# An earlier branch in a four-layer kernel's second layer, its planes' loads on three queues, and a gate product ahead of a reciprocal in the third

## The chip, the cores and the metric

The kernel runs on one core of one Trainium2 chip. Its engines are TensorE (PE, with its weight loads shown apart as PEld), VectorE (DVE), ScalarE (ACT), GpSimd (POOL) and SyncE (SP)[...]; SP, ACT and POOL also issue DMAs. The metric is the device time of one execution, in microseconds. Times come from three runs; the profile is of one further execution.

## What is computed

The input x is an image of 256 x 256 pixels with 128 channels, f32. Four layers are added to it one after the other, each on the group-normalised image:

```python
x = x + _L0_conv_ref(_gn(x), ...)   # triangle attention, 4 heads, gated
x = x + _L1_conv_ref(_gn(x), ...)   # triangle multiplication, 16 planes
x = x + _L2_conv_ref(_gn(x), ...)   # triangle multiplication, 128 planes
x = x + _L3_conv_ref(_gn(x), ...)   # shifts, taps and pixel-wise products
```

The change touches the second and the third of these (called layer 1 and layer 2 here, as in the code):

```python
def _L1_conv_ref(x, ...):
    a = jax.nn.sigmoid((x @ Wa1 + ba1) * (x @ Wa2 + ba2))
    b = jax.nn.sigmoid((x @ Wb1 + bb1) * (x @ Wb2 + bb2))
    g = jax.nn.sigmoid(x @ Wg + bg)
    z = jnp.einsum('bikc,bkjc->bijc', a, b)
    return g * (_ln(z, ln2_g, ln2_b) @ Wz + bz)

def _L2_conv_ref(z, ...):
    zn = _layernorm(z, ln_in_w, ln_in_b)
    a = jax.nn.sigmoid(zn @ Wga + bga) * (zn @ Wla + bla)
    b = jax.nn.sigmoid(zn @ Wgb + bgb) * (zn @ Wlb + blb)
    k = jnp.einsum('bimc,bmjc->bijc', a, b)
    return jax.nn.sigmoid(zn @ Wgo + bgo) * (_layernorm(k, ln_o_w, ln_o_b) @ Wlo + blo)
```

## The kernel before

Channels lie on the 128 partitions. The image is cut into 32 chunks (NSC) of 2048 pixels (SC), one f32 tile of 1 MB each; a chunk has four pieces of 512 pixels (CK). Between layers, x lies in DRAM (x1T after layer 0, x2T after layer 1, x3T after layer 2). Within the loops that matter here the order of instructions on each engine is the order in which the code issues them (`tc.manual_schedule()`).

Layer 1 has a first pass over all chunks (pool p3, line 944 on). `order1` (line 598) gives the order of the chunks. Every chunk has two sets of four matmuls of 128 x 32 by 512 (`piece_ab`, line 931, matmuls on line 937), an ACT addition (line 941), a DVE product (line 942), an ACT sigmoid (line 950), and one store of 256 KB into abD (line 951) that is issued one chunk later by POOL; the last chunk's is issued by SP. abD holds the 16 a planes and 16 b planes. The x tiles come from x1T on SP (`load1`, line 878, its DMA on line 881): eight chunks are there from layer 0, ten (NEAR) are loaded into left-hand slots before the pass, ten (FAR) into right-hand slots once the attention's memory is given up at the ninth chunk, and the last four reuse left-hand slots as soon as their chunks are done. So SP issues the load of the last chunk after the twelfth chunk's turn. Of the right-hand slots, seven (k from 3 to 9, `over_scope`) are given up at the end of the pass. Thirteen tiles (SLOTS, those of `order4[:SLOTS]`) stay in memory for layer 1's last pass (p4), which goes through the chunks in `order4`; that order is derived from `order1` by the list `after`.

After the pass comes a branch (lines 975 and 976): a flag, computed well before, says whether the statistics of layer 0 are usable. If they aren't, a general version of the attention is run, all chunks are done again, and the thirteen resident tiles are loaded anew; with these inputs this arm isn't taken. The branch is taken by all engines, each on its own.

Then the planes' products (pool z): for every pair of planes g, `load_z` reads A in four DMAs of 128 KB (line 1012) and B in two of 256 KB (line 1016) from abD. All are issued by SP, but for g = 0 ACT issues the two of B. PE transposes A's planes (line 2049) and multiplies (line 2060). The statistics over planes, layer 1's normalisation and the last pass follow.

Layer 2 computes its a and b planes into DRAM, and then the 128 products (p6): per plane, PE transposes and multiplies, ACT copies and squares, DVE adds to the sum k1 (line 1434), and POOL to the sum of squares k2 (line 1435). Its closing stage (p7, from line 1463) first makes the reciprocal standard deviation of k per pixel: k1 squared and scaled (line 1533, DVE), k2 + k1 (line 1534, DVE), max with 0 (line 1535, DVE), square root (line 1536, ACT), reciprocal (line 1537, DVE), a store of it to rkD and four loads of it as rows rk. Per chunk, a gate in two halves (`gate7`): two matmuls of 128 x 128 by 512 into a PSUM tile `p7_pm` of two buffers (line 1490), DVE adds a column and multiplies with rs2's row broadcast over partitions (line 1500), ACT takes the sigmoid. The broadcast (`spread_z`, line 1481, POOL's partition_broadcast on line 1484) has two buffers. The gates of chunks 0 to 2 stand ahead of the loop; `spread_k(0)` and `normalise_k` scale the first chunk of k, and in the loop PE does the gate three chunks ahead and the product of this chunk's k.

Of the kernel before, what the change touches and what calls it, by code (L numbers as in the profile page):

```python
# [8 lines left out]
F32 = mybir.dt.float32  # L9
AF = mybir.ActivationFunctionType  # L10
# [21 lines left out]
def kernel(ctx: ExitStack, tc: tile.TileContext, a: dict, out: bass.AP):  # L32
# [562 lines left out]

    order1 = [14, 15, 0, 16, 1, 17, 30, 31] + [b + h * NSC // 2 for b in range(2, NSC // 2 - 2) for h in range(2)]
    xs = {}

    def fill1(s, x):
# [265 lines left out]

    NEAR, FAR, FIRST = 10, 10, 8  # L870
    SLOTS = 13
    x1_scope, far_scope = ExitStack(), ExitStack()
    near = [
# [51 lines left out]
    usum = const.tile([P, 2 * NSC], F32, name="usum")  # L925
    qsum = const.tile([P, NSC], F32, name="qsum")

    after = [16, 17, 14, 15, 22, 23, 28, 29, 30, 31, 12, 13, 24, 25, 2, 3, 4, 5, 8, 9, 10, 11, 0, 6, 1, 7, 18, 19, 20, 21, 26, 27]
    order4 = [order1[i] for i in after]

    with x1_scope, far_scope:
# [10 lines left out]
            nc.vector.scalar_tensor_tensor(s1, p2, vb2, s1, ALU.add, ALU.mult)  # L942
            return s1, sb.tile([P, CK], F32, name="p3_ab", bufs=5)

        with tc.tile_pool(name="p3", bufs=2, reuse_waits="tile") as sb, tc.tile_pool(name="p3ps", bufs=3, space=PSUM, reuse_waits="tile") as ps, tc.manual_schedule():
            open_ab = []

            def close3(queue):
                s, s1, ab = open_ab.pop(0)
                nc.scalar.activation(ab, s1, AF.Sigmoid)  # L950
                queue.dma_start(abD[:, s * CK : (s + 1) * CK], ab)

            for i, s in enumerate(order1):
                if i == FIRST:
                    att_scope.close()
                    far = [
                        far_scope.enter_context(tc.tile_pool(name=f"x1_r{k}", bufs=1, side="right", reuse_waits="tile"))
                        for k in range(3)
                    ]
                    over_scope = ExitStack()  # L960
                    far += [
                        over_scope.enter_context(tc.tile_pool(name=f"x1_r{k}", bufs=1, side="right", reuse_waits="tile"))
                        for k in range(3, FAR)
                    ]
                    for m, k in enumerate((9, 4, 3, 8, 1, 0, 2, 7, 6, 5)):
                        load1(order1[FIRST + NEAR + m], far[k])
                open_ab.append((s, *piece_ab(s, sb, ps)))
                if i + NEAR + FAR < NSC and i >= FIRST:
                    load1(order1[i + NEAR + FAR], home[s])
                if i:  # L970
                    close3(nc.gpsimd)
            close3(nc.sync)
        over_scope.close()

        again = nc.values_load(flag[0:1, 0:1], min_val=0, max_val=1)
        with tc.If(again > 0):
            general_attention(
                tc, dict(xT=xT, rsD=rsD, mbD=mbD, triD=triD, x1T=x1T),
                dict(wf=wf, wo=wo, b_g=b_g, b_o=b_o, cqkg=cqkg, cv=cv, mneg=mneg, ident=ident),
                dram, stats1,  # L980
            )
            nc.vector.bn_aggr(mv1, stats1.rearrange("p n s -> p (n s)"))
            weights1("gn1g")
            with tc.tile_pool(name="g3", bufs=2, reuse_waits="tile") as sb, tc.tile_pool(name="g3ps", bufs=2, space=PSUM, reuse_waits="tile") as ps:
                held = dict(xs)
                for s in order1:
                    xs[s] = sb.tile([P, SC], F32, name="g3_x")
                    nc.sync.dma_start(xs[s], x1T[:, s * SC : (s + 1) * SC])
                    s1, ab = piece_ab(s, sb, ps)
                    nc.scalar.activation(ab, s1, AF.Sigmoid)  # L990
                    nc.sync.dma_start(abD[:, s * CK : (s + 1) * CK], ab)
                xs.update(held)
            for s in order4[:SLOTS]:
                nc.sync.dma_start(xs[s], x1T[:, s * SC : (s + 1) * SC])

# [3 lines left out]
        with tc.tile_pool(name="z", bufs=2, reuse_waits="tile") as sb, tc.tile_pool(name="zps", bufs=3, space=PSUM, reuse_waits="tile") as ps, tc.manual_schedule():  # L999
# [6 lines left out]
            def load_z(g):  # L1006
                if g < 8:
                    ab = gate_pool.tile([P, 4, 2 * N], F32, name="z_ab", tag="g")
                    AB[g] = A, B = ab[:, 0:2, :], ab[:, 2:4, :]
                    for q in range(4):  # L1010
                        r = slice(32 * q + 2 * g, 32 * q + 2 * g + 2)
                        nc.sync.dma_start(
                            A[32 * q : 32 * q + 32, :, :], abD[r, :].rearrange("c (s t) -> s c t", t=CK)
                        )
                    for c in range(2):
                        (nc.sync if g else nc.scalar).dma_start(
                            B[:, c, :], abD.rearrange("(q c) (s t) -> c s q t", q=4, t=CK)[16 + 2 * g + c]
                        )

# [372 lines left out]

    k1 = rk_pool.tile([P, 2 * N], F32, name="k1")
    k2 = rk_pool.tile([P, 2 * N], F32, name="k2")
    xs7 = {}

    def load7x(s):
        if s < NSC:
# [3 lines left out]
    with tc.tile_pool(name="p6", bufs=3, reuse_waits="tile") as sb, tc.tile_pool(name="p6ps", bufs=3, space=PSUM, reuse_waits="tile") as ps:  # L1402
        nc.vector.memset(k1, 0.0)
        nc.gpsimd.memset(k2, 0.0)  # L1404
        with tc.manual_schedule():
            quads = {}

            def load6(q):
                if q < D // 4:
                    A = sb.tile([P, 4, 2 * N], F32, name="p6_A")  # L1410
                    nc.sync.dma_start(A, aD[:, 4 * q : 4 * q + 4, :])
                    B = sb.tile([P, 4, 2 * N], F32, name="p6_B")
                    nc.sync.dma_start(B, bD[:, 4 * q : 4 * q + 4, :])
                    quads[q] = A, B

            def turn6(c):
                return tri_turn(nc, ps, sb, quads[c // 4][0], c % 4, ident, nc.vector.tensor_copy)

            for q in range(3):
                load6(q)  # L1420
            for s in range(4):
                load_row7(s)
            at = turn6(0)
            for c in range(D):
                q = c // 4
# [8 lines left out]
                nc.vector.tensor_tensor(k1, pz, k1, ALU.add)  # L1434
# [25 lines left out]
    g1 = const.tile([P, NSC + 1], F32, name="g1")  # L1460
    g2 = const.tile([P, NSC + 1], F32, name="g2")
    with tc.tile_pool(name="p7", bufs=2, reuse_waits="tile") as sb, tc.tile_pool(name="p7psX", bufs=2, space=PSUM, reuse_waits="tile") as psX, tc.tile_pool(name="p7psM", bufs=2, space=PSUM, reuse_waits="tile") as psM, tc.manual_schedule():
        ks, rks, rbs, gts = {}, {}, {}, dict(gates)
        junk = sb.tile([P, SC], F32, name="p7_junk", bufs=1)
        AHEAD = 3

# [14 lines left out]
        def spread_z(s):  # L1481
            if s < NSC and s not in gates:
                rbs[s] = sb.tile([P, SC], F32, name="p7_rb")
                nc.gpsimd.partition_broadcast(rbs[s], row7(s))

        def product7(src, w, h):
            pm = psM.tile([P, 2, CK], F32, name="p7_pm")
# [46 lines left out]
        nc.vector.tensor_tensor(k2, k2, k1, ALU.add)  # L1534
        nc.vector.tensor_scalar(k2, k2, 0.0, None, ALU.max)
        nc.scalar.activation(k2, k2, AF.Sqrt, bias=epst, scale=1.0 / D)
        nc.vector.reciprocal(k1, k2)
# [15 lines left out]
        for s in range(NSC):  # L1553
# [3 lines left out]
            for h in range(2):  # L1557
# [5 lines left out]
                )  # L1563
                if h == 0:
                    spread_k(s + 1)
                    spread_z(s + AHEAD + 1)
# [535 lines left out]
```

## The time and profile before

| what | us |
| --- | --- |
| median of three runs | 3238.36 |
| the runs | 3231.83, 3238.36, 3238.47 |
| the profiled execution | 3235.55 |
| its span, first to last instruction | 3233.8 |
| PE busy | 3052.5 (94%) |
| DVE busy | 2266.3 (70%) |
| ACT busy | 2035.2 (63%) |
| POOL busy | 1742.1 (54%) |

Layer 1's first pass begins at 1469.50 in the profile, its last store is issued at 1541.98, and the first planes' transposes begin at 1553.00. Layer 2's last plane product ends at 2596, and the closing stage's first matmul of the loop's steady work stands at 2620.33.

In the profile's lines, a time in front is the start in microseconds from the span's start, then the duration, the engine, the line of the code and the operation, what is written from what (output arrow input, with shapes), and how many instructions the line joins. A bracket gives the engine's idle time just ahead of it, and what ended that: the engine and instruction, or the DMA, that it waited for. An engine with a q (SPq) is its sequencer: DMA issues, branches and semaphore events, which don't count as busy. The mean granted TensorE clock over the span was 0.971 of full speed.

### The profile page before, as it was taken

Reading aid. Unit: us, or ns where it says so; the run is one execution under the profiler, and the core shown is the slowest. Engines: PE = TensorE matmul, PEld = TensorE weight load, DVE = VectorE, ACT = ScalarE, POOL = GpSimd, SP = SyncE. Lnnn points to the kernel's source line nnn. Section 1 sums busy time; section 2 is a strip of 40 time slices with the busy share of each in tenths; the row PEclk is TensorE's granted clock in tenths of the full one; section 3 lists DMA queues with packets and bytes.
Section 4 is the critical chain, followed back from the end, with each engine's and each line's share of the span. In section 5 each row is a group of like instructions: output and inputs, shape, how many; then the busy total and the mean of one; then the engine's idle time right before and its main releaser. Section 6 shows DMA issues by size and latency. Waiting matters only on the chain. (4 is left out here: it accounts for less than half of the span.)

```text
span 3233.8 us, 51742 instructions
## 1 busy us (share of the span) xinstructions
PE 3052.5 (94%) x19916; PEld 1629.4 (50%) x19916; DVE 2266.3 (70%) x2633; ACT 2035.2 (63%) x2275; POOL 1742.1 (54%) x951
## 2 busy tenths in 40 slices
PE   5699999999999999998798899999999989979998
PEld 4535555555555555552533344444699933324444
DVE  5657888888888888884456454455455578858887
ACT  3577777777777777764477544444344457757776
POOL 4006777777777777771277000000255568858887
PEclk8899999999999999999998899999999999989999
DMA  9973333333333333349589687676799989986885
GB/s 373 408 293 96 113 120 113 106 123 116 106 114 118 113 113 119 113 156 422 173 317 382 242 297 298 237 270 253 268 352 351 344 316 388 387 298 196 236 237 155
DMA packets 289526, 746.18 MB, mean 231 GB/s; under 512 B 68473, under 2 KB 139019, under 8 KB 240987
## 3 DMA queue, kind: packets, MB, share of 16 engines
q1 hardware_dynamic: 276881, 717.12, 62.1%
q0 software_dynamic: 8976, 23.49, 1.9%
q8 instruction: 159, 2.61, 0.3%
q10 hardware_dynamic: 3416, 2.19, 0.3%
q14 instruction: 94, 0.77, 0.1%
HBM read 455.26 MB, written 287.45 MB: 230 GB/s over the span
## 5 line engine op out<-in xcount | busy, mean ns | idle before, releaser
L679 POOL TENSOR_TENSOR p_es<-p_e 128x1024 f32<-128x1024 f32 x256 | 603.7, 2369 | 318.8 <-DMA p_x<-xT 195.7
L669 DVE TENSOR_TENSOR p_e<-p_S,tri_raw 128x1024 f32<-128x1024 f32 x512 | 609.4, 1212 | 143.4 <-PE p_S L659 142.0
L677 ACT ACTIVATE p_e<-p_e,mbT 128x1024 f32<-128x1024 f32 x512 | 552.1, 1138 | 62.1 <-DVE p_e L669 62.0
L1281 PE MATMUL p_pm<-p_zn,wf 128*128 128x512 f32 x1040 | 450.4, 595 | 1.9 <-ACT p_a L1342 1.9
L644 PE MATMUL p_mm<-p_xn,w 128*128 128x512 f32 x764 | 404.3, 612 | 0.1
L1281 PEld LDWEIGHTS p_pm<-p_zn,wf 128*128 128x128 f32 x1040 | 197.4, 190 | 255.0 <-issue 248.1
L659 PE MATMUL p_S<-p_qk 32*128 32x256 f32 x4096 | 295.4, 400 | 3.3 <-DVE p_e L669 3.3
L1404 POOL MEMSET k<- 128x512 f32 x1 | 0.5, 527 | 517.9 <-PE p_pm L1281 517.9
L659 PEld LDWEIGHTS p_S<-p_qk 32*128 32x128 f32 x4096 | 185.9, 184 | 159.2 <-PE p_mm L635 91.7
L2060 PE MATMUL tp_z<-p_B,tp_at 128*128 128x256 f32 x1024 | 250.6, 388 | 1.0 <-DVE tp_at L2051 1.0
L692 PE MATMUL p_o<-p_e,p_vg 128*32 128x256 f32 x4096 | 248.9, 384 | 0.0
L626 POOL TENSOR_TENSOR p_xn<-p_xn,p_rs 128x1024 f32<-128x1024 f32 x62 | 148.9, 2402 | 180.7 <-DMA p_rb<-rzD 119.6
L1435 POOL TENSOR_TENSOR k<-k,p_sq 128x512 f32<-128x512 f32 x128 | 163.2, 1275 | 136.4 <-ACT p_sq L1433 136.4
L2060 PEld LDWEIGHTS tp_z<-p_B,tp_at 128*128 128x128 f32 x1024 | 185.3, 191 | 23.7 <-DVE tp_at L2051 1.8
L1434 DVE TENSOR_TENSOR k<-tp_z,k 128x512 f32<-128x512 f32 x128 | 88.6, 692 | 127.5 <-ACT p_sq L1433 127.5
L644 PEld LDWEIGHTS p_mm<-p_xn,w 128*128 128x128 f32 x764 | 125.1, 190 | 103.6 <-issue 87.2
L692 PEld LDWEIGHTS p_o<-p_e,p_vg 128*32 128x32 f32 x4096 | 120.4, 110 | 110.4 <-ACT p_vg L650 41.5
L650 ACT ACTIVATE p_vg<-p_mm,bgh 128x512 f32<-128x512 f32 x128 | 88.0, 687 | 135.0 <-PE p_mm L644 135.0
L1431 ACT COPY p_K<-tp_z 128x512 f32<-128x512 f32 x128 | 75.0, 586 | 155.4 <-PE tp_z L2060 155.4
L1346 DVE SCALAR_TENSOR_TENSOR p_b<-p_pm,b2w,p_b 128x1024 f32<-128x1024 f32 x64 | 82.2, 1284 | 124.7 <-PE p_pm L1281 110.3
L635 PEld LDWEIGHTS p_mm<-w,p_xn 128*128 128x128 f32 x1016 | 133.9, 192 | 61.3 <-issue 60.6
L648 ACT ACTIVATE p_qk<-p_mm,cqkg 128x512 f32<-128x512 f32 x127 | 87.5, 689 | 122.5 <-PE p_mm L644 122.3
(417 smaller groups left out, 6094.0 us busy)
## 6 DMA issues: line engine op xcount, KB each, us to landing
p_x<-x2T SPq DMA_DIRECT2D x57, 1024.0 KB
x<-x1T SPq DMA_DIRECT2D x47, 1024.0 KB
p_x<-in_x_dram SPq DMA_DIRECT2D x32, 1024.0 KB
p_x<-xT SPq DMA_DIRECT2D x64, 512.0 KB
p_rs<-rsD SPq DMA_DIRECT2D x64, 512.0 KB
x2T<-x SPq DMA_DIRECT2D x32, 1024.0 KB
aD<-p_a SPq DMA_DIRECT2D x32, 1024.0 KB
bD<-p_b SPq DMA_DIRECT2D x32, 1024.0 KB
```

The source lines that it names most:

```text
L626: nc.gpsimd.tensor_tensor(xn, xn, groups[g]["rs"], ALU.mult)
L635: nc.tensor.matmul(pm[:, k * D : (k + 1) * D], lhsT=t["xn"][:, b * P : (b + 1) * P], rhs=wf[:, 2 * D : 3 * D], start=True, stop=True,)
L644: nc.tensor.matmul(pm, lhsT=w, rhs=t["xn"][:, cs_], start=True, stop=True)
L659: nc.tensor.matmul(Ss[h // 2][:, h % 2, u, :], lhsT=t["k"][hp, r * N + u * P : r * N + (u + 1) * P], rhs=t["q"][hp, r * N : (r + 1) * N], ...
L669: nc.vector.tensor_tensor(e[:, :, 2 * p : 2 * p + 2, :].rearrange("p u h n -> p h u n"), Ss[p], triT[:, 2 * p : 2 * p + 2, :, :], ALU.add,)
L677: nc.scalar.activation(e[:, u, :, :], e[:, u, :, :], AF.Exp, bias=mbT[:, u, i : i + 1])
L679: nc.gpsimd.tensor_tensor(es, e[:, 0, :, :], e[:, 1, :, :], ALU.add)
L692: nc.tensor.matmul(t["o"][hp, r % 2, :], lhsT=t["v"][:, r * 2 + u, hp], rhs=e[:, u, h, :], start=(u == 0), stop=(u == 1),)
L1281: nc.tensor.matmul(pm[:, c, :], lhsT=wf2[:, i, :], rhs=zns[s][:, k * CK : (k + 1) * CK], start=True, stop=True)
L1434: nc.vector.tensor_tensor(k1, pz, k1, ALU.add)
L1435: nc.gpsimd.tensor_tensor(k2, k2, sq, ALU.add)
L2060: nc.tensor.matmul(pz[:, t, :], lhsT=at[:, u, t * P : (t + 1) * P], rhs=Bc[:, u, :], start=(u == 0), stop=(u == 1))
```

## The change

- The order of chunks in layer 1's first pass: 30 and 31 change places with 1 and 17. The list `after` and the order in which the right-hand slots are filled are changed with it.
- The first pass becomes a function `pass_a(lo, hi, queue)`. It is called for the first 25 chunks (TAIL = NSC − 7), whose last store POOL issues; then the slots of `over_scope` are given up, the flag is read and the branch is taken; then it is called for the last seven chunks, whose last store SP issues. The arm that isn't taken repeats only the first 25 chunks, and loads the thirteen resident tiles anew as before.
- For g = 0 the planes' loads are spread: A's first two on SP, A's other two on ACT, B's two on POOL.
- Layer 2's closing stage: the first broadcast is made inside the plane loop, 16 planes before its end, in a buffer of its own, and the broadcasts then alternate between that buffer and one of the stage's. k2 + k1 goes from DVE to POOL, max with 0 from DVE to ACT as a Relu; the gate's first half for chunk 0 is put ahead of the reciprocal, its second half just behind it.

```diff
-    order1 = [14, 15, 0, 16, 1, 17, 30, 31] + [b + h * NSC // 2 for b in range(2, NSC // 2 - 2) for h in range(2)]
+    order1 = [14, 15, 0, 16, 30, 31, 1, 17] + [b + h * NSC // 2 for b in range(2, NSC // 2 - 2) for h in range(2)]
...
-    NEAR, FAR, FIRST = 10, 10, 8
+    NEAR, FAR, FIRST, TAIL = 10, 10, 8, NSC - 7
...
+        with tc.tile_pool(name="p3", bufs=2, reuse_waits="tile") as sb:
+            def pass_a(lo, hi, queue):
+                with tc.tile_pool(name=f"p3ps_{lo}", bufs=3, space=PSUM, reuse_waits="tile") as ps, tc.manual_schedule():
+                    open_ab = []
...
+                    for i in range(lo, hi):
+                        s = order1[i]
+                        if i == FIRST:
...
+                            for m, k in enumerate((9, 4, 3, 8, 7, 6, 5, 2, 1, 0)):
+                                load1(order1[FIRST + NEAR + m], far[k])
+                        open_ab.append((s, *piece_ab(s, sb, ps)))
+                        if i + NEAR + FAR < NSC and i >= FIRST:
+                            load1(order1[i + NEAR + FAR], home[s])
+                        if i > lo:
+                            close3(nc.gpsimd)
+                    close3(queue)
+
+            far, over_scope = [], ExitStack()
+            pass_a(0, TAIL, nc.gpsimd)
+            over_scope.close()
+            again = nc.values_load(flag[0:1, 0:1], min_val=0, max_val=1)
+            with tc.If(again > 0):
+                general_attention(
...
+                    for s in order1[:TAIL]:
...
+                for s in order4[:SLOTS]:
                     nc.sync.dma_start(xs[s], x1T[:, s * SC : (s + 1) * SC])
...
+            pass_a(TAIL, NSC, nc.sync)
...
-                        nc.sync.dma_start(
+                        (nc.sync if g or q < 2 else nc.scalar).dma_start(
                             A[32 * q : 32 * q + 32, :, :], abD[r, :].rearrange("c (s t) -> s c t", t=CK)
                         )
                     for c in range(2):
-                        (nc.sync if g else nc.scalar).dma_start(
+                        (nc.sync if g else nc.gpsimd).dma_start(
...
+    rb_pool = rs2_scope.enter_context(tc.tile_pool(name="rb7", bufs=1, side="right", reuse_waits="tile"))
...
+    def spread_z(s, pool):
+        if s < NSC and s not in gates:
+            rbs[s] = pool.tile([P, SC], F32, name="p7_rb", bufs=1)
+            nc.gpsimd.partition_broadcast(rbs[s], row7(s))
...
                 nc.gpsimd.tensor_tensor(k2, k2, sq, ALU.add)
+                if c == D - 16:
+                    spread_z(0, rb_pool)
...
-        spread_z(0)
-        spread_z(1)
-
         nc.vector.scalar_tensor_tensor(k1, k1, -1.0 / D, k1, ALU.mult, ALU.mult)
-        nc.vector.tensor_tensor(k2, k2, k1, ALU.add)
-        nc.vector.tensor_scalar(k2, k2, 0.0, None, ALU.max)
+        nc.gpsimd.tensor_tensor(k2, k2, k1, ALU.add)
+        nc.scalar.activation(k2, k2, AF.Relu)
         nc.scalar.activation(k2, k2, AF.Sqrt, bias=epst, scale=1.0 / D)
+        spread_z(1, sb)
+        gate7(0, 0)
         nc.vector.reciprocal(k1, k2)
+        gate7(0, 1)
...
         for s in range(3):
-            gate7(s, 0)
-            gate7(s, 1)
+            if s:
+                gate7(s, 0)
+                gate7(s, 1)
             if s < 2:
-                spread_z(s + 2)
+                spread_z(s + 2, (rb_pool, sb)[s % 2])
```

More of the change, by code (lines that the diff above doesn't have):

```diff
@@ L926 @@
     qsum = const.tile([P, NSC], F32, name="qsum")
-    after = [16, 17, 14, 15, 22, 23, 28, 29, 30, 31, 12, 13, 24, 25, 2, 3, 4, 5, 8, 9, 10, 11, 0, 6, 1, 7, 18, 19, 20, 21, 26, 27]
+    after = [16, 17, 14, 15, 26, 27, 28, 29, 30, 31, 12, 13, 25, 24, 2, 3, 6, 7, 8, 9, 10, 11, 0, 4, 1, 5, 18, 19, 20, 21, 22, 23]
     order4 = [order1[i] for i in after]
@@ L943, in piece_ab @@
             return s1, sb.tile([P, CK], F32, name="p3_ab", bufs=5)
[L945 to L987, printed above, removed]
-                    nc.sync.dma_start(xs[s], x1T[:, s * SC : (s + 1) * SC])
[L989 to L994, printed above, removed]
+        with tc.tile_pool(name="p3", bufs=2, reuse_waits="tile") as sb:
+            def pass_a(lo, hi, queue):
+                with tc.tile_pool(name=f"p3ps_{lo}", bufs=3, space=PSUM, reuse_waits="tile") as ps, tc.manual_schedule():
+                    open_ab = []
+                    def close3(queue):
+                        s, s1, ab = open_ab.pop(0)
+                        nc.scalar.activation(ab, s1, AF.Sigmoid)
+                        queue.dma_start(abD[:, s * CK : (s + 1) * CK], ab)
+                    for i in range(lo, hi):
+                        s = order1[i]
+                        if i == FIRST:
+                            att_scope.close()
+                            for k in range(FAR):
+                                scope = far_scope if k < 3 else over_scope
+                                far.append(scope.enter_context(
+                                    tc.tile_pool(name=f"x1_r{k}", bufs=1, side="right", reuse_waits="tile")
+                                ))
+                            for m, k in enumerate((9, 4, 3, 8, 7, 6, 5, 2, 1, 0)):
[12 more added lines that the diff above has]
+                general_attention(
+                    tc, dict(xT=xT, rsD=rsD, mbD=mbD, triD=triD, x1T=x1T),
+                    dict(wf=wf, wo=wo, b_g=b_g, b_o=b_o, cqkg=cqkg, cv=cv, mneg=mneg, ident=ident),
+                    dram, stats1,
+                )
+                nc.vector.bn_aggr(mv1, stats1.rearrange("p n s -> p (n s)"))
+                weights1("gn1g")
+                with tc.tile_pool(name="g3", bufs=2, reuse_waits="tile") as sb_g, tc.tile_pool(name="g3ps", bufs=2, space=PSUM, reuse_waits="tile") as ps:
+                    held = dict(xs)
+                    for s in order1[:TAIL]:
+                        xs[s] = sb_g.tile([P, SC], F32, name="g3_x")
+                        nc.sync.dma_start(xs[s], x1T[:, s * SC : (s + 1) * SC])
+                        s1, ab = piece_ab(s, sb, ps)
+                        nc.scalar.activation(ab, s1, AF.Sigmoid)
+                        nc.sync.dma_start(abD[:, s * CK : (s + 1) * CK], ab)
+                    xs.update(held)
+                for s in order4[:SLOTS]:
+                    nc.sync.dma_start(xs[s], x1T[:, s * SC : (s + 1) * SC])
+            pass_a(TAIL, NSC, nc.sync)
@@ L1394 @@
     k2 = rk_pool.tile([P, 2 * N], F32, name="k2")
-    xs7 = {}
+    xs7, rbs = {}, {}
+    def spread_z(s, pool):
+        if s < NSC and s not in gates:
+            rbs[s] = pool.tile([P, SC], F32, name="p7_rb", bufs=1)
+            nc.gpsimd.partition_broadcast(rbs[s], row7(s))
     def load7x(s):
@@ L1462 @@
     with tc.tile_pool(name="p7", bufs=2, reuse_waits="tile") as sb, tc.tile_pool(name="p7psX", bufs=2, space=PSUM, reuse_waits="tile") as psX, tc.tile_pool(name="p7psM", bufs=2, space=PSUM, reuse_waits="tile") as psM, tc.manual_schedule():
-        ks, rks, rbs, gts = {}, {}, {}, dict(gates)
+        ks, rks, gts = {}, {}, dict(gates)
         junk = sb.tile([P, SC], F32, name="p7_junk", bufs=1)
@@ L1479, in normalise_k @@
                 nc.vector.tensor_tensor(ks[s][:, hs], rks[s][h], ks[s][:, hs], ALU.mult)
[L1481 to L1484, printed above, removed]
         def product7(src, w, h):
@@ L1565 @@
                     spread_k(s + 1)
-                    spread_z(s + AHEAD + 1)
+                    spread_z(s + AHEAD + 1, (rb_pool, sb)[s % 2])
                 normalise_k(s + 1, h)
```

## The prediction

> **What bounds the kernel now.** I read the page first: PE is busy 94% of the 3233.8 us span, so a change in the order of work can only win where PE stands still. The table of windows then priced the two stages that the change touches, and the timelines of both showed which wait ends last. The table's columns are PE, PEld, DVE, ACT and POOL busy with their counts, then granted clock, DMA share and GB/s:
>
> ```profile
> 1469.50:1517.00 47.50, 46.91 (x400) 11.87 (x400) 16.73 (x24) 29.89 (x45) 11.41 (x21) 0.94 1.02 422
> 1517.00:1542.00 25.00, 13.47 (x112) 3.48 (x112) 7.43 (x10) 12.66 (x20) 5.43 (x11) 1.00 0.85 351
> 1542.00:1553.00 11.00, 0.00 (x1) 0.03 (x1) 0.48 (x1) 0.00 (x0) 0.00 (x0) 0.56 0.66 176
> 2597.90:2609.50 11.60, 3.75 (x9) 1.49 (x9) 10.64 (x7) 2.66 (x4) 5.97 (x3) 0.80 0.96 364
> 2620.30:2700.00 79.70, 79.70 (x240) 31.22 (x237) 71.16 (x60) 54.75 (x52) 61.76 (x19) 1.00 0.94 362
> ```
>
> Layer 1's first pass has its inputs early up to 1517. Its last seven chunks go at the pace of the loads (13.47 us of PE in 25), and then comes an 11 us hole. Layer 2's closing stage opens with PE at 3.75 of 11.60 us; after that PE is full. The end of layer 1's pass:
>
> ```profile
> 1535.32 1.92 PE L937 MATMUL p<-x,v 128*32 128x512 f32 x16 [1.63 <-DMA x<-x1T]
> ...
> 1538.51 1.92 PE L937 MATMUL p<-x,v 128*32 128x512 f32 x16 [1.27 <-DMA x<-x1T]
> ...
> 1541.33 0.63 ACT L950 ACTIVATE p_ab<-p_s 128x512 f32<-128x512 f32 x1 [0.43 <-DVE p_s L942]
> 1541.98 0.33 SPq L951 DMA_DIRECT2D abD<-p_ab  x1
> 1546.22 1.24 ACTq L1016 DMA_DIRECT2D z_ab<-abD  x2
> 1546.28 0.48 DVE L1026 MEMSET z_Z<- 128x512 f32 x1 [4.99 <-SPq L976]
> 1546.71 3.95 SPq L1012 DMA_DIRECT2D z_ab<-abD  x8
> ...
> 1553.00 1.95 PE L2049 MATMUL tp_a<-ident,z_ab 128*128 128x128 f32 x8 [12.57 <-DMA z_ab<-abD]
> ```
>
> Each chunk waits for its own load, the last computes at once, and then the branch and the planes' loads stand alone: 1541.96 to 1553.00 is 11.04 us. The view of the branch's line says what SP does in it:
>
> ```profile
> L976 SPq EVENT_SEMAPHORE  x8: 17/17/17, 1545.5 to 1546.1; - x8
> L976 PEldq COMPARE_BRANCH  x1: 3416/3416/3416, 1539.2 to 1539.2; - x1
> ...
> L976 SPq COMPARE_BRANCH  x1: 50/50/50, 1542.4 to 1542.4; - x1
> ```
>
> Eight semaphore events of SP follow its branch: one for each of its eight DMA counters. In the closing stage of layer 2:
>
> ```profile
> 2597.95 3.70 PE L1490 MATMUL p_pm<-p_x,wf 128*128 128x512 f32 x8 [1.90 <-DVE k L1434]
> 2598.56 5.30 POOL L1484 PARTITION_BROADCAST p_rb<-rs__18576  x2
> 2599.24 2.47 DVE L1534 TENSOR_TENSOR k<-k,k 128x512 f32<-128x512 f32 x1
> 2601.74 2.41 DVE L1535 TENSOR_SCALAR k<-k 128x512 f32<-128x512 f32 x1
> ...
> 2604.93 3.35 DVE L1537 RECIPROCAL k<-k 128x512 f32<-128x512 f32 x1 [0.79 <-ACT k L1536]
> 2608.20 2.38 DVE L1500 SCALAR_TENSOR_TENSOR p_g<-p_pm,gcol,p_rb 128x1024 f32<-128x1024 f32 x2
> ...
> 2609.45 9.88 PE L1490 MATMUL p_pm<-p_x,wf 128*128 128x512 f32 x16 [7.79 <-DVE p_g L1500]
> ```
>
> PE has two gate products and no free PSUM buffer; DVE gets to their release only behind the reciprocal, so PE idles 7.79 us.
>
> [...] chunks took 3.42 us each at the pass's start (1469.50 to 1475.2) and 1.72 when warm (two chunks, 1482.52 to 1485.95). [...] here eight issues took SP 3.95 us. [...]
>
> **Part 1, the branch seven chunks earlier.** Meant: branch and events hidden under the loads. But the program of the changed kernel, built and not run, has this in the arm not taken: SP waits for all DMAs that it has issued, on each of its eight counters, and only then adds what the other arm would have counted. Line 881 issues the last x load at 1510.3, before the branch, so the wait covers the last load. And PE's first matmul of chunk 25 waits for a counter's value *after* that addition, since the other arm loads the resident x tiles anew. So chunks 25 to 31 can't start with their own loads; all wait until the last has landed. Queued behind SP's wait: only the last ab store and the planes' loads, later anyway.
>
> - Last load: before, 1538.4 (PE starts at 1538.51). The stalled chunks put two or three ab stores of 256 KB fewer ahead of it; at 422 GB/s each is 0.62 us, 1.2 to 1.9 in all. I take 1536.9.
> - Burst of seven chunks: 7 × 1.72 = 12.0 us. PE has stood idle about 20 us and starts cold: 5.7 us at 3.42 a chunk do what 2.85 do warm, 2.85 more. ACT needs 0.69 + 0.63 = 1.32 a chunk, less than PE. PE ends at 1551.8, the last ab, 1.5 later as before, at about 1553.4 instead of 1541.96: **+11.4**. Bounds: +9 if the load comes earlier and PE warms sooner, +13 if the load is as late as before.
>
> **Part 2, planes on three queues, after the branch.** Of the 11.04 us, the branch goes (last store to first plane load was 4.24 us at ACT; a lone store lands 2.3 us after issue by its line's view, so about 2.0 of it is branch). Three issuers with two loads each instead of SP's first four in 2.0 us and more save 1.0 to 1.6. I take 11.04 − 3.5 = **7.5 us, −3.5**; bounds −2 and −4.5. Layer 1 nets +7.9.
>
> **Part 3, the closing stage.** The two broadcasts lay beneath DVE's 2.47 and 2.41; the same forms undisturbed took 0.69 (L1052) and 0.43 (L1054). One moves into the product loop: 2.3 to 2.65 us of POOL, whose slack is 2.27 − 1.27 = 1.0 an iteration with three buffers to lag in: nothing, +1 if not. Chain now: DVE's first product ends 2599.13; POOL's add 1.27 (L1435) in place of 2.47; ACT's Relu about 0.63 (128x512, L950) in place of 2.41; sqrt's table load 1.28, formerly hidden (it began at 2597.20), now lies behind Relu at worst; sqrt 0.72; reciprocal. It ends about 2606.6 instead of 2608.28. The first gate half goes on DVE at 2600.05, frees a PSUM buffer, and PE does the third half product early; the second goes at 2606.6 to 2607.85. PE restarts there, instead of at 2609.45, with three half products done instead of two (one cold: about 1.7). Together −3.3; PE is full afterwards (the row from 2620.30), so this reaches the end. Bounds −2 (Relu and tables slower, cold anyway) and −6.5 (clock stays warm). What is late next: the reciprocal's row through DRAM, store to use; it lands about 2612.5, before its use at some 2616.0, so nothing.
>
> The swap in order1, the derived orders and far slots exchange equal loads: nothing; the loads cover them (DMA share 1.02). If an order made one chunk of layer 1's closing stage late, up to +2.
>
> **Sum.** +11.4 − 3.5 − 3.3 = **+4.6 us**. On the profiled execution, 3235.55 us (span 3233.8 and 1.75 around it), that is 3240.2; the median of the runs is 3238.36, 2.81 above it, so 3243.0. The kernel's measurements can tell about 0.2% from no change, 6.5 us.
>
> **Rivals.**
> - *Slower: the second planes land late on POOL's queue.* In the DMA view POOL's 256 KB issues take 9.0 (ab stores) and 10.6 us (p_z) to land, ACT's z loads came within 6.9 of issue. Against it: those were taken on saturated queues, here DMA is nearly idle. It decides once a landing exceeds 6.9 us: 2 to 4.3 us more for the first product, +8.9 in all with the rest, 3247.3. Chance 0.27.
> - *The seven chunks do stream with their loads*, the wait of SP not holding PE. For it: before, each chunk waited for its own load alone. Against it: the counters' values in the built program. Then only −3.5 and −3.3: −6.8, 3231.6. Chance 0.10.
> - *The clock stays warm in the closing stage, or the burst starts sooner.* PE's longest idle there falls to about 4.65 us[...]. +1 to +2 net, about 3239.8. Chance 0.11.
>
> **How the numbers follow.** Forecast 0.52: 3243.0, by its bounds 3238 to 3247. Range: down to 3234, between the third and second rivals, up to 3250 for the first rival with late ends. Within 0.2% (3231.9 to 3244.8) I put 0.40 of the forecast's 0.52, 0.02 of the first rival, 0.05 of the second and 0.06 of the third: 0.53. Slower: 0.10 of the forecast and 0.25 of the first rival, 0.35. Faster: 0.02 of the forecast, half of the second rival, and 0.05 of the third, since the runs before themselves reach down to 3231.83: 0.12.
>
> **What would show it.** In the changed trace PE should stand idle from about 1516 to 1537 in the pass, then do seven chunks without a wait; if each of the last seven again names its x load, part 1 is wrong. From the last ab to the first plane product should be 7 to 8 us; over 9, with POOL's load as releaser, is the first rival. In the closing stage a gate half stands before the reciprocal and PE restarts 1.6 us earlier; if the first broadcast delays the product loop, or a table load stands twice, part 3 is smaller. Wrong altogether: a change in the stages outside these two of over 2 us.

## The result, and the profile after

| | before | changed |
| --- | --- | --- |
| median of 20 runs, us | 3235.55 | 3242.62 |
| lowest and highest, us | 3229.11, 3241.39 | 3233.97, 3246.82 |
| profiled execution, us (span) | 3235.55 (3233.8) | 3233.97 (3231.8) |

The ratio of changed to before is 1.0019, with a 95% interval from 1.0013 to 1.0026: 4.2 to 8.4 us slower. With twenty runs the kernel before has a median 2.81 us lower than with the three that were known at first. And the changed kernel's profile is of the quickest of its twenty executions. So the two spans must not be set against each other; stages are.

I take two distances inside each trace, since everything that the change touches lies in them: from the first pass's first matmul to the first planes' transposes, and from the start of the last matmul of layer 2's plane products to the first broadcast of rk's rows. Before, they are 83.5 and 23.6 us. In the changed kernel they are 91.1 and 20.2: **+7.6 and −3.4, +4.2 together**.

What PE waited for in the changed kernel between 1500 and 1560 us (engine, tile and line waited with, what ended it, us in all, times, longest):

```profile
PE p L937 <- SPq L977: 20.9, 1, 20.9
PE tp_a L2055 <- DMA z_ab<-abD: 8.0, 1, 8.0
```

In place of many short waits for x there is one of 20.9 us, and the profile names SP's branch as what ended it. The windows of the changed kernel, in the columns used before:

```profile
1465.80:1518.70 52.90, 46.82 (x400) 11.83 (x400) 18.88 (x26) 33.19 (x50) 12.52 (x24) 0.92 1.02 421
1518.70:1533.90 15.20, 0.03 (x4) 0.06 (x5) 0.00 (x0) 0.63 (x1) 1.06 (x2) 0.50 0.84 347
1533.90:1548.90 15.00, 14.98 (x112) 4.17 (x112) 4.51 (x6) 7.47 (x13) 2.71 (x5) 0.81 0.19 72
1548.90:1556.90 8.00, 0.00 (x0) 0.02 (x1) 1.24 (x2) 1.08 (x2) 1.64 (x3) 0.77 0.66 215
```

25 chunks (400 matmul records; the trace has two for each of a chunk's eight matmuls), then nothing on PE while the loads still run at 347 GB/s, then seven chunks in one go (112 records in 15.0 us) while the loads are over (72 GB/s). The 15.2 us of the second row are the part of PE's wait behind its own branch; the wait of 20.9 us begins at 1513.0. Loads and matmuls, which lay beside each other before, now stand one behind the other. The second row's granted clock is 0.50, and the burst's mean 0.81: 0.50 in its first 5.40 us (28 records) and 0.99 in the other 9.60 (88). Such a slow start is called cold below, also where an experiment's times alone show it. The branch's own line in the changed kernel:

```profile
L977 SPq EVENT_SEMAPHORE  x8: 17/17/17, 1516.8 to 1534.1; - x8
L977 SPq COMPARE_BRANCH  x1: 50/50/50, 1507.5 to 1507.5; - x1
L977 PEldq COMPARE_BRANCH  x1: 6272/6272/6272, 1512.5 to 1512.5; - x1
```

SP branches at 1507.5, but the last of its eight counters is settled at 1534.1, 26.6 us later. The first five events lie 3.5 to 3.7 us apart, the pace at which the loads let the chunks through before; the last three stand at 1533.6 to 1534.1, when the loads are over (16 and 33 GB/s in the two half microseconds from 1532.0, nothing from 1533.0 on). PE starts at 1533.87, behind the seventh. The closing stage in the changed kernel's timeline:

```profile
2596.07 1.20 DVE L1535 SCALAR_TENSOR_TENSOR k<-k 128x512 f32<-128x512 f32 x1
...
2597.41 1.26 POOL L1536 TENSOR_TENSOR k<-k,k 128x512 f32<-128x512 f32 x1 [0.69 <-DVE k L1535]
2598.16 1.28 DVE L1505 SCALAR_TENSOR_TENSOR p_g<-p_pm,gcol,p_rb 128x1024 f32<-128x1024 f32 x1 [0.90 <-PE p_pm L1495]
2598.70 0.63 ACT L1537 ACTIVATE k<-k 128x512 f32<-128x512 f32 x1 [3.40 <-POOL k L1536]
...
2599.35 1.28 ACT L1538 ACT_TABLE_LOAD   x1
...
2601.47 3.35 DVE L1541 RECIPROCAL k<-k 128x512 f32<-128x512 f32 x1 [2.02 <-ACT k L1538]
...
2605.98 8.05 PE L1495 MATMUL p_pm<-p_x,wf 128*128 128x512 f32 x12 [4.48 <-DVE p_g L1505]
```

The half gate stands ahead of the reciprocal. In place of DVE's steps of 2.47 and 2.41 us there are POOL's of 1.26 and ACT's Relu of 0.63, with no table load ahead of the Relu. PE pauses 4.48 us instead of 7.79, with 12 matmul records left to do behind the pause instead of 16.

### The profile page after: what moved, and what is told of

Read it like the earlier page. It is cut to its first block, busy times and chain, and to the rows that moved or that the text cites. A ratio compares the mean times of both kernels' runs of the same rounds, so it can differ in the third digit from the quotient of the medians.

```text
span 3231.8 us, 51747 instructions
## 1 busy us (share of the span) xinstructions
PE 3048.1 (94%) x19916; PEld 1627.6 (50%) x19916; DVE 2260.7 (70%) x2631; ACT 2037.6 (63%) x2276; POOL 1743.2 (54%) x954
## 3 DMA queue, kind: packets, MB, share of 16 engines
q10 hardware_dynamic: 3288, 1.93, 0.2%
## 5 line engine op out<-in xcount | busy, mean ns | idle before, releaser
L659 PE MATMUL p_S<-p_qk 32*128 32x256 f32 x4096 | 295.1, 400 | 3.3 <-DVE p_e L669 3.3
```

The costliest lines, as they stand in the source:

```text
L659: nc.tensor.matmul(Ss[h // 2][:, h % 2, u, :], lhsT=t["k"][hp, r * N + u * P : r * N + (u + 1) * P], rhs=t["q"][hp, r * N : (r + 1) * N], ...
```

## The experiments

The first two columns are the two distances in each kernel's trace, the third what they add up to against the kernel before (83.5 + 23.6); the last is the ratio of runs to those of the kernel before on the same chip. At some 3233 us, 0.001 is 3.2 us. Kernels without a ratio were run once, so that only their traces are read. e1 and e5 leave out reloads that the arm that isn't taken needs; they serve as experiments only.

| kernel | pass to planes | planes to rk | sum against before | ratio, 95% interval |
| --- | --- | --- | --- | --- |
| changed | 91.1 | 20.2 | +4.2 | 1.0019 (1.0013 to 1.0026) |
| e1_noreload | 83.6 | 19.2 | −4.3 | 0.9988 (0.9978 to 0.9997) |
| e2_arm_on_pool | 89.2 | 19.2 | +1.3 | 1.0013 (1.0004 to 1.0021) |
| e3_tail31 | 83.5 | 19.2 | −4.4 | 0.9988 (0.9982 to 0.9995) |
| e4_closing_stage_only | 83.5 | 19.2 | −4.4 | 0.9983 (0.9975 to 0.9990) |
| e5_noreload_own_ab | 81.5 | 19.2 | −6.4 | 0.9986 (0.9979 to 0.9993) |
| e6_layer1_only | 91.1 | 23.6 | +7.6 | 1.0032 (1.0022 to 1.0041) |
| e7_branch_behind_pass | 82.4 | 19.2 | −5.5 | 0.9988 (0.9979 to 0.9997) |
| e8_tail28 | 85.7 | 19.2 | −2.2 | |
| e9_order_only | 83.3 | 23.5 | −0.3 | 1.0001 (0.9993 to 1.0010) |
| e10_two_queues | 96.3 | 19.2 | +8.4 | 1.0041 (1.0027 to 1.0055) |
| e11_no_lead_gate | 83.3 | 21.1 | −2.7 | |
| e12_planes_as_before | 92.2 | 19.2 | +4.3 | |

**e1_noreload: what does PE wait for, the branch or a merged counter?**

```diff
-                for s in order4[:SLOTS]:
-                    nc.sync.dma_start(xs[s], x1T[:, s * SC : (s + 1) * SC])
             pass_a(TAIL, NSC, nc.sync)
```

> The changed kernel with the arm that is not taken left without its thirteen reloads of the resident x tiles (that arm alone would compute with old tiles). SP's wait on its eight counters in the branch stays. Theory (PE waits for counter values that only the branch's addition reaches, because the arm reloads tiles of the last seven chunks): each of the last seven chunks waits for its own load again; from the pass's first matmul to its last about 70 us as before, instead of 82.5; first planes' product about 79.5 us after the pass's start instead of 91.1 (83.5 before); against the kernel before -4 there and -3.4 in the closing stage, -7.4 us or 0.9977. Rival (the branch itself holds PE until SP is through it, whatever the arm contains): PE stands idle for 15 us before the seven chunks as in the changed kernel, ratio 1.0019.

83.6 us instead of the expected 79.5. The theory's direction holds, but of the 11.6 us that it set against the changed kernel 7.5 came, and the timeline says why:

```profile
1526.46 10.74 PE L937 MATMUL p<-x,v 128*32 128x512 f32 x80 [10.24 <-DVEq L977]
1537.72 0.63 ACT L952 ACTIVATE p_ab<-p_s 128x512 f32<-128x512 f32 x1 [5.72 <-SPq L977]
```

PE is no longer held by SP's branch: it starts the last chunks at 1526.46, once DVE is through its own branch, and does five of them (80 matmuls). But now ACT waits for SP's branch, before the first sigmoid of the last seven chunks. The arm that isn't taken takes its ab tiles from the pass's pool and stores them by SP; so the next user of such a tile waits for a counter value that only SP's branch brings. The merged wait sat in two places, and I had seen one.

**e5_noreload_own_ab: both taken away.**

```diff
-                        s1, ab = piece_ab(s, sb, ps)
+                        s1, ab = piece_ab(s, sb_g, ps)
```

(on top of e1's edit; the arm's pool `sb_g` was there already for its x tiles)

> The kernel of e1_noreload (the arm not taken does without its thirteen reloads), and that arm takes its ab tiles from a pool of its own, so that no store of that arm stands between ACT and the pass's ab tiles. Theory (every tile that the arm's DMAs touch too makes its next user wait for SP's whole branch): ACT no longer stops for about 6 us before the sigmoids of the last seven chunks; the pass streams; first planes' product 79 to 80 us after the pass's start (83.6 in e1, 91.1 in the changed kernel, 83.5 before); -4 there and -4.3 in the closing stage, about -8 us against the kernel before, 0.9975. Rival (ACT was held by the branch itself): as e1, 83.6 us and 0.9988.

```profile
1527.71 14.36 PE L937 MATMUL p<-x,v 128*32 128x512 f32 x112 [10.59 <-DVEq L977]
```

All seven chunks now go without a stop, and ACT's 5.72 us are gone: SP's branch holds nobody, though its last counter is settled only at 1538.2. That is 81.5 us, 9.6 less than the changed kernel, against 79 to 80 expected: PE still stands idle for 10.59 us; in that time PE's own branch takes 6.23 us and DVE's next event comes 5.6 us after its branch (last section). From the last ab store's issue (1543.63) to the planes' transposes (1552.19) are 8.6 us (7.8 in e1) where the changed kernel took 6.5; I didn't follow that up.

**e2_arm_on_pool: the same wait moved to another engine.**

```diff
-            nc.sync.dma_start(...)      # all DMAs of general_attention and of the arm's chunks and reloads
+            nc.gpsimd.dma_start(...)
```

> The changed kernel with all DMAs of the arm that is not taken issued by POOL instead of SP. Theory: SP has nothing to wait for in the branch, POOL waits for its own ab stores, the last of which lands about 9 us after its issue; PE gets chunk 25 about 4 us earlier than in the changed kernel and does a burst whose end is set by its own length: first planes' product about 87 us after the pass's start instead of 91.1, +0 to +1 us against the kernel before (1.000 to 1.0005). Rival (the branch itself holds PE until the last x load): no change from the changed kernel, 1.0019.

89.2 us where 87 was expected. SP has no waits in the branch any more; PE's idle time before the burst is 19.40 us, and POOL's ab stores are named as what ended it:

```profile
1533.03 14.21 PE L937 MATMUL p<-x,v 128*32 128x512 f32 x112 [19.40 <-DMA abD<-p_ab]
```

```profile
L977 POOLq EVENT_SEMAPHORE  x4: 17/43/43, 1522.4 to 1528.7; - x4
...
L977 POOLq INC_SWDGE_SEM  x1: 2131/2131/2131, 1530.8 to 1530.8; - x1
```

POOL issued its last store ahead of the branch at 1521.13, and the pass's ab stores by POOL take 9.0 us to land at the median and at most 9.9 in the changed kernel's trace, so by estimate it was there between 1530 and 1531. At 1530.8 POOL begins the 2.13 us of its INC_SWDGE_SEM, and PE starts 0.1 us after their end. So PE seems to have waited for POOL's branch as it waited for SP's before, and these 2.13 us, which the expectation had not counted, are the 2.2 that it missed. By the traces of the two kernels, the issuer of the DMAs of an arm that was not taken decided whose outstanding DMAs the following work waited for: SP's for 20.9 us, POOL's for 19.4.

**e3_tail31 and e8_tail28: how many chunks stand behind the branch.**

```diff
-    NEAR, FAR, FIRST, TAIL = 10, 10, 8, NSC - 7
+    NEAR, FAR, FIRST, TAIL = 10, 10, 8, NSC - 1
```

(NSC − 4 in e8_tail28)

> The changed kernel with one chunk behind the branch instead of seven. Theory: the chunks before the branch stream with their loads, the last one waits for the last load, which it needs anyway; nothing is left of the burst, PE's own branch of 3.4 us delays the last chunk by about 2; first planes' product about 80.5 us after the pass's start (91.1 in the changed kernel, 83.5 before); with the closing stage -6 us against the kernel before, 0.9981. Rival (the cost lies in the branch's place among the loads, not in the number of chunks behind it): still about 90 us, ratio 1.0015 to 1.002.

> The changed kernel with four chunks behind the branch instead of seven. Theory (burst behind the last load, cold at first): the four chunks start about 68.5 us after the pass's start and take about 9.7 instead of 15.0 us; first planes' product about 86 us after the pass's start. Rival (the wait doesn't depend on the number of chunks): 89 to 91 us.

Seven, four and one chunk behind the branch give 91.1, 85.7 and 83.5: the cost shrinks with what stands behind the branch. e8's distance came as expected (86), its course not quite. The first of its four chunks waits for DVE's branch alone and starts 64.1 us after the pass's start, cold (3.64 us, where a chunk ahead of the branch took 1.92); only the last three wait for SP's counters and go in one burst (70.5 us after the pass's start, 7.05 us long). e3 missed by 3 us (80.5 expected), because the branch comes back at the end:

```profile
1546.96 3.39 PE L937 MATMUL p<-x,v 128*32 128x512 f32 x16 [4.53 <-ACTq L977]
```

The last chunk waits 4.53 us for ACT's way through the branch, and runs cold (3.39 us, against 1.92 or 1.93 for the chunks ahead). The branch was not hidden; it moved ahead of one chunk. A chunk of e3 that stands ahead of the branch warns of the profile's label:

```profile
1530.02 1.93 PE L937 MATMUL p<-x,v 128*32 128x512 f32 x16 [1.46 <-SPq L977]
```

PE's own branch stands at 1541.5, and so this chunk can't wait for it; it waits for its load, whose landing lets SP's branch (events from 1526.5 to 1544.1) go on at the same time. So the label alone doesn't tell a wait for SP's branch from one for a load; e1 does.

**e4_closing_stage_only and e6_layer1_only: each half alone.**

e4 is the kernel before with the diff's second half, e6 the changed kernel with that half taken back:

```diff
+                if c == D - 16:
+                    spread_z(0, rb_pool)
...
-        nc.vector.tensor_tensor(k2, k2, k1, ALU.add)
-        nc.vector.tensor_scalar(k2, k2, 0.0, None, ALU.max)
+        nc.gpsimd.tensor_tensor(k2, k2, k1, ALU.add)
+        nc.scalar.activation(k2, k2, AF.Relu)
...
+        gate7(0, 0)
         nc.vector.reciprocal(k1, k2)
+        gate7(0, 1)
```

> The kernel before with the closing stage's part of the change alone. Theory: from the last plane product to the first broadcast of rk's rows 20.2 us instead of 23.6, and all of it reaches the end: -3.4 us, 0.9990. Rival (the gain is given back in the loop behind it, which PE or the loads of x bound): 0.9998 to 1.0002.

> The changed kernel with the closing stage of layer 2 as before. Theory: first planes' product 91.1 us after the pass's start instead of 83.5, +7.6 us against the kernel before, 1.0023. Rival (the medians of the changed kernel, +7.07, and of the closing stage alone, -5.5, differ by 12.6, so some 4 to 5 us more lie in other stages, from the new order of chunks): +11 to +12.6 us, 1.0034 to 1.0039, with a stage outside these two that is 4 us longer.

e4 gains 4.4 us in its stage, and 0.0017 (5.5 us) by the runs: the gain reaches the end. The stage is at 19.2 us in every other kernel with the whole of this closing stage; the changed kernel's own profile, at 20.2, is the exception (what PE does behind its pause took 8.05 us there and 7.11 in e4). e6 loses 7.6 us in its stage; 1.0032 is 10.3 us, with 7.1 to 13.3 in the interval, so its lower end holds the stage's loss and the rival's 11 to 12.6 is not excluded by the runs (e9 tests the rival's reason). The halves are opposite in sign, and the larger is the loss.

**e9_order_only: is there a third part?**

```diff
-    order1 = [14, 15, 0, 16, 1, 17, 30, 31] + ...
+    order1 = [14, 15, 0, 16, 30, 31, 1, 17] + ...
```

(with the new `after` and the new order of the right-hand slots)

> The kernel before with the new order of chunks alone (order1, after, the order of the right-hand slots). Theory (the order costs nothing): 83.5 us from the pass's start to the first planes' product, all other stages as before, ratio 1.0000 within 0.0007. Rival (the medians of the changed kernel and of e6 stand some 3 us above what the two stages' traces add up to, because the new order lengthens another stage): +3 us, 1.0009, the taps of layer 3 at 287 us instead of 284.

1.0001 (0.9993 to 1.0010), both distances as before within 0.3 us: nothing, by the median; the interval just reaches the rival's 1.0009. Layer 3's taps took 286.5 us here, but 286.1 in e11, which has the old order, and 282.9 in e3, which has the new one, so that stage's length doesn't go with the order.

**e7_branch_behind_pass and e12_planes_as_before: the loads on three queues.**

e7 is the kernel before with the new closing stage and this; e12 the changed kernel without this:

```diff
-                        nc.sync.dma_start(
+                        (nc.sync if g or q < 2 else nc.scalar).dma_start(
                             A[32 * q : 32 * q + 32, :, :], abD[r, :].rearrange("c (s t) -> s c t", t=CK)
...
-                        (nc.sync if g else nc.scalar).dma_start(
+                        (nc.sync if g else nc.gpsimd).dma_start(
```

> The kernel before, its branch behind all chunks and its order of chunks, with the first planes' loads on three queues and the new closing stage. Theory: the planes' loads are issued 4.2 us after the last ab store as before, and land 4.2 us later as in the changed kernel instead of 6.3: first planes' product 81 to 81.5 us after the pass's start (83.5 before), -2.3 there and -4.3 in the closing stage, -6.6 us, 0.998. Rival (the split of the loads gains nothing[...]): 83.5 us, -4.3 to -5.5 us, 0.9985.

> The changed kernel with the first planes' loads as before, A on SP and B on ACT. Theory: from the last ab store's issue to the first planes' product 7.5 to 8 us instead of 6.5, first planes' product about 92.3 us after the pass's start instead of 91.1. Rival ([...] the split is worth nothing): 91.1 us.

In e12 the last ab store is issued at 1554.42, and then:

```profile
1556.68 4.43 SPq L1014 DMA_DIRECT2D z_ab<-abD  x8
1556.70 1.24 ACTq L1018 DMA_DIRECT2D z_ab<-abD  x2
...
1563.19 1.95 PE L2055 MATMUL tp_a<-ident,z_ab 128*128 128x128 f32 x8 [10.33 <-DMA z_ab<-abD]
```

8.8 us from store to product, against 6.5 in the changed kernel: three issuers save 2.3 us there. (The whole distance differs by 1.1, 92.2 against 91.1, since e12's burst took 14.15 us and not 15.01.) Behind the branch (e7) they save 1.1, 82.4 instead of 83.5, less than the 2 to 2.5 expected. Both traces say that the split gains, against the rivals; e7's runs (0.9988) can't tell the theory's 0.998 from the rival's 0.9985.

**e11_no_lead_gate: what the leading half gate is worth.**

```diff
-        gate7(0, 0)
         nc.vector.reciprocal(k1, k2)
+        gate7(0, 0)
         gate7(0, 1)
```

> e4_closing_stage_only with the first half gate of chunk 0 put back behind the reciprocal. Theory (the lead half lets PE do one half product more before its pause): from the last plane product to the first broadcast of rk's rows about 20.7 us instead of 19.3 (23.6 before): the half product, cold, is 1.4 to 1.7 of the 4.3, the shorter chain to the reciprocal the rest. Rival (the lead half is the whole gain): 23 us or more. Other rival (it is nothing): 19.3.

21.1 us against 19.2 with it and 23.6 before. First e11's restart of PE, then e4's:

```profile
2607.63 8.95 PE L1493 MATMUL p_pm<-p_x,wf 128*128 128x512 f32 x16 [6.19 <-DVE p_g L1503]
```

```profile
2606.61 7.11 PE L1493 MATMUL p_pm<-p_x,wf 128*128 128x512 f32 x12 [4.48 <-DVE p_g L1503]
```

PE restarts at the same distance from its first product (9.9 us) in both, so the lead half doesn't shorten the chain; it moves four of the trace's matmul records from behind the pause to before it. By this one execution, 1.9 of the 4.4 us are the half gate, and 2.5 the shorter chain to the reciprocal. In that chain the broadcasts have moved and two steps have gone to other engines at once; which of the two is worth how much was not taken apart.

**e10_two_queues: an attempt at a complete kernel that streams.**

```diff
-                            close3(nc.gpsimd)
+                            close3(nc.sync if 17 <= i < TAIL else nc.gpsimd)
...
-            pass_a(0, TAIL, nc.gpsimd)
+            pass_a(0, TAIL, nc.sync)
...
-                        s1, ab = piece_ab(s, sb, ps)
+                        s1, ab = piece_ab(s, sb_g, ps)
...
-                    nc.sync.dma_start(xs[s], x1T[:, s * SC : (s + 1) * SC])
+                    (nc.gpsimd if s in order1[TAIL:] else nc.sync).dma_start(xs[s], x1T[:, s * SC : (s + 1) * SC])
```

> The changed kernel, complete in both arms: the arm not taken keeps its reloads, but those of the last seven chunks' tiles are issued by POOL, its ab tiles have a pool of their own, and SP issues the ab stores of chunks 16 to 24, so that POOL has nothing late to wait for in its branch. Theory: PE, ACT and DVE wait for nothing that SP's branch holds; the last seven chunks start once the branch is through on all engines, as in e5; first planes' product 81.5 us after the pass's start (91.1 in the changed kernel, 83.5 before), -2 there and -4.3 in the closing stage, -6.3 us, 0.9981. Rival (SP's branch holds them all the same, by a wait not thought of): 89 to 91 us, 1.001 to 1.002.

96.3 us, the slowest of all. The idea fell on its own edit:

```profile
1517.33 41.93 SPq L953 DMA_DIRECT2D abD<-p_ab  x10
...
1535.49 0.63 ACT L952 ACTIVATE p_ab<-p_s 128x512 f32<-128x512 f32 x1 [17.28 <-DMA abD<-p_ab]
...
1542.38 14.97 PE L937 MATMUL p<-x,v 128*32 128x512 f32 x112 [23.06 <-DVEq L977]
```

SP issues its first ab store at 1517.33, behind the x loads of its own queue, and ACT gets that tile back only at 1535.49, 18.2 us later. So ACT, DVE behind it, and with them the branch, came late. Whether the waits it meant to remove were gone can't be read from it; what shows the theory is e5, and this run is a warning about SP's queue.

No kernel here has a lower ratio than e4, the kernel before with the closing stage alone: 0.9983. e7's trace promises 1.1 us more; the runs can't tell the two apart.

## Why the prediction was right

The forecast was 3243.0, the median is 3242.62, and +4.6 was the sum of its steps where the two traces show +4.2. Two things were luck. The level was reached from a median of three runs that was 2.81 us too high, while by the medians the change cost 7.07, about as much more than the sum. And the traces of the four timed kernels that stay later than before in the pass all add up to less than their runs show (+4.2, +1.3, +7.6, +8.4 against about +6, +4, +10, +13). I looked for this difference in the order of chunks (e9) and did not find it; a trace is one execution, and stages that the kernels share differ between executions by as much (the attention from 1202.7 to 1207.6 us, layer 3's taps from 282.9 to 289.4). One pattern points to layer 3 all the same. From the first to the last transpose of its line 1811 (up to six lines further down in the other kernels), the five traces whose planes start late (changed, e2, e6, e10, e12) take 294.6 to 297.7 us, the nine others 291.8 to 295.1, 2.6 less in the mean; and PE's longest sum of waits there, before and then changed, is

```profile
PE p_pm L1774 <- DVE p_pb L1782: 2.0, 2, 1.3
```

```profile
PE p_pm L1780 <- DVE p_pb L1788: 6.0, 8, 1.3
```

(3.8 to 6.1 in the five, 2.0 to 4.4 in the nine). What would carry a delay in layer 1 that far, no run shows. The cause stays open.

By its steps:

- *The last load.* Forecast 67.4 us after the pass's start (1536.9 − 1469.5); PE was released at 68.1. That is 0.9 us earlier than the last chunk before (69.0), where 1.5 was forecast; that the missing stores brought it is not shown.
- *PE waits for the last load, through the other arm's counters.* Shown by e1 and e5, which take the common tiles away and set PE and ACT free while SP's branch is as late as ever (its last counter settled at 1537.6 in e1 and 1538.2 in e5); the wait of 20.9 us and its label fit. The forecast said that SP's waits stand in the arm not taken; they stand on the path that is run when that arm is skipped, as SP's eight events behind its branch show. It named only x's tiles; the ab tiles carried the same wait, which stayed hidden behind it until e1. And "all wait until the last has landed" is a shade too strong: PE went behind the seventh of eight events here (1533.87, the eighth at 1534.1), and e8's first chunk started at 1534.20, with SP's last event at 1540.6.
- *The burst.* Forecast 14.9 us with 2.85 for the cold clock; it was 15.01. The granted clock was 0.50 for 5.40 us (28 records) after PE's 20.9 us idle; at the pass's start before it was 0.52 for 5.70 us (28 records). The last ab store was issued 84.7 us after the pass's start, 12.2 later than before; +11.4 was forecast.
- *The planes.* Forecast −3.5, measured 11.04 to 6.5, −4.5. Branch and split were worth 2.3 each (8.8 in e12, run once, between them), where 2.0 and 1.0 to 1.6 had been set. With the step before, +7.6 where +7.9 was forecast: the two misses cancel.
- *The first rival* (planes late on POOL's queue) did not come: POOL issued at 1553.20, and the product started 3.7 us later.
- *The closing stage.* Forecast −3.3, −3.4 in the changed kernel's trace and −4.4 in the others with all of it. The reciprocal ended 8.75 us after the start of DVE's first product (forecast 8.7), PE paused 4.48 us (4.65). What differed between executions is how soon PE was fast again, the bound of the step: behind the pause its weight loads start about 0.85 us apart for 5.3 us in the changed kernel's trace (granted clock 0.50) and for 3.3 in e4's, then 0.47 and 0.43 apart in the first (0.99), 0.63 and 0.43 in the second. The third rival's warm clock did not come: a pause of 4.48 us was enough for 0.50; from what length on the clock falls is not shown.
- *The sign to look for that was too strict*: changes of over 2 us in other stages appear in this very pair of traces (the attention −3.3, the taps +3.1) although the sizes of the steps were nearly right.

## What to carry to other kernels

Of the kernels here with seven chunks behind the branch, the one whose following work shared no DMA-touched tile with the arm that isn't taken was the only one quicker to the planes than before (81.5 us in e5, 83.5 before, 91.1 in the changed kernel), and even there PE stood idle for 10.6 us at the branch. Ask, for each engine behind it, which tile the untaken arm's DMAs touch, and which queue must catch up before that tile is free. The answer stood in the program's waits before any run. And a gain in one stage and a loss in another can stand in one diff; take each alone, as the closing stage here was worth keeping and the branch's move was not.

## What the runs showed of the hardware

A branch was dear on PE here, and dearer among the loads. First a kernel with its branch at the end of the pass (e7), then one with it among the loads (e5):

```profile
L976 PEldq COMPARE_BRANCH  x1: 3948/3948/3948, 1543.0 to 1543.0; - x1
```

```profile
L977 PEldq COMPARE_BRANCH  x1: 6232/6232/6232, 1516.6 to 1516.6; - x1
```

In the changed kernel it was 6272 ns and before 3416. In three traces where PE's branch stands at the end of the loads (before, e3, e7) it took 3.4 to 3.9 us, in six where it stands among them (changed, e1, e2, e5, e8, e10) 5.9 to 6.4; that the full DMA engines are the reason was not tested. DVE's branch lasts 72 ns in all nine, but its next event came 2.9 us later before (1541.2 to 1544.1) and 5.5 later in the changed kernel (1518.1 to 1523.6). Where no counter of SP's holds PE, 10.2 (e1) and 10.6 us (e5) still pass without a matmul around its branch, until DVE's event. POOL, where it had DMA counts to make up in the branch, spent 2.13 (e2) and 1.94 us (e10) on one instruction, INC_SWDGE_SEM. And a store issued behind loads on SP's queue was back after 18.2 us (e10), where the changed kernel's stores by POOL in the same pass land in 9.0 at the median.
